# Group coefficients of the next channels between the halves of a product, and GpSimd's circuit work behind them

## The chip, the cores and the metric

The kernel runs on one core of a Trainium2 chip. The metric is the device time of one execution in microseconds (us); lower is better. Engines are named as in the profile: PE is TensorE (matmuls; PEld its weight loads), DVE is VectorE, ACT is ScalarE, POOL is GpSimd, and SP is the engine that issues most of the loads. L299 is line 299 of the kernel.

## The reference

Four residual layers are applied to x of shape (4, 512, 32, 32), each on a group-normalized input: attention with mixed heads, a gate per channel from a small simulated circuit of rotations, a second attention, and a look-up in a memory of 2048 rows. The change concerns the first normalization and the first product of layer 0, for image 0, and constants of the circuit of layer 1.

```python
def _gn(v, G=32, eps=1e-5):
    g = v.reshape(B_, G, C_ // G, H_, W_)            # 32 groups of 16 channels
    m = jnp.mean(g, axis=(2, 3, 4), keepdims=True)
    s = jnp.var(g, axis=(2, 3, 4), keepdims=True)
    return ((g - m) / jnp.sqrt(s + eps)).reshape(v.shape)

# layer 0
x = x + _L0_conv_ref(_gn(x), ...)
#   in it: q = einsum('oc,bct->bot', w_q, xf), likewise k and v, then attention
# layer 1: y = mean of _gn(x) over the positions of each channel; 2 layers of
#   9 rotations on the 512 amplitudes of y; gate = sigmoid(q_out @ fc_w.T + fc_b)
```

Image 0 is 512 channels by 1024 positions. In the kernel the channels lie in four chunks (KC = 4) of 128 partitions. A group is 16 channels, so the coefficients of a chunk depend on that chunk alone: its products can start when its own coefficients are known.

## The kernel before

The group coefficients come from a generator in four pieces. `pin` keeps an instruction in program order with the other pinned ones; what isn't pinned may be placed elsewhere in its engine's queue by the scheduler. `small_ps` is always the same PSUM bank, shown as pt.

```python
def rsqrt(dst, src):                         # GpSimd, L124
    nc.gpsimd.tensor_tensor(dst, src, mhalf[...], ALU.pow)

def group_coeffs_parts(mean, var, tag):
    ps = small_ps(f"gps_{tag}")
    pin(nc.tensor.matmul(ps[:, 0:n], gavg, mean, start=True, stop=True))    # L140
    gm = tile_("gm")
    pin(nc.vector.tensor_copy(gm, ps[:, 0:n]))                              # L142
    yield
    dm, sq = tile_("dm"), tile_("gsq")
    nc.gpsimd.tensor_sub(dm, mean, gm)                                      # L145
    nc.gpsimd.tensor_mul(sq, dm, dm)                                        # L146
    nc.gpsimd.tensor_add(sq, sq, var)                                       # L147
    yield
    ps2 = small_ps(f"gps2_{tag}")
    pin(nc.tensor.matmul(ps2[:, 0:n], gavg, sq, start=True, stop=True))     # L150
    ve = tile_("gve")
    pin(nc.vector.tensor_scalar_add(ve, ps2[:, 0:n], GN_EPS))               # L152
    yield
    rstd = tile_("grstd")
    rsqrt(rstd, ve)                                                         # L124
    yield gm, rstd, dm
```

The first image, with the chunks of x and of w_q loaded in turn:

```python
def first():
    # ... loads of xn[:, k], w_q[:, k], then w_k and w_v
    def stats(k):
        for i in range(2):
            pin(nc.vector.bn_stats(st[:, i, :], xn[:, k, i * NB:(i + 1) * NB]))   # L292
        pin(nc.vector.bn_aggr(mv, ...))                                           # L293
        parts[k] = group_coeffs_parts(mv[:, 0:1], mv[:, 1:2], f"a0_{k}")

    def normalize(k):
        next(parts[k])                       # second matmul, + eps
        gm, rstd, dm = next(parts[k])        # power
        pin(nc.vector.tensor_scalar(xn[:, k, :], xn[:, k, :], gm, rstd,
                                    ALU.subtract, ALU.mult))                      # L299
        nc.gpsimd.tensor_mul(ybar[:, k:k + 1], dm, rstd)                          # L301

    def multiply(k):
        for m in range(2):
            for n in range(T // NB):
                pin(nc.tensor.matmul(pairs[f"mx{m}"][:, n, :],                    # L306
                    w[:, k, m * P:(m + 1) * P], xn[:, k, n * NB:(n + 1) * NB],
                    start=(k == 0), stop=(k == KC - 1)))

    stats(0)
    next(parts[0])
    next(parts[0])                           # mean; deviation and its square
    for k in range(KC):
        if k + 1 < KC:
            stats(k + 1)
        normalize(k)
        if k + 1 < KC:
            next(parts[k + 1])
            next(parts[k + 1])
        multiply(k)
    for m in range(2):
        put_q(q, m)(flat2(pairs[f"mx{m}"]))  # ScalarE copies q out, L272
    for m, at in ((2, "sc"), (3, "mx0")):
        project(w, tokens(xn), m, at, put_q(q, m))       # matmuls at L183
```

The multiplication of a chunk with w_q fills two pairs of PSUM banks, mx0 and mx1, with four matmuls of 512 columns; each shows as two instructions in the profile. The rest of q follows at L183, and then k, in the banks mx1, sc, mx0, mx1 (DVE copies k out, L373), v and the attention steps.

```python
first()
circuit()
for m, at in enumerate(("mx1", "sc", "mx0", "mx1")):
    take_k(0, m, at)
```

`circuit()` makes constants for layer 1. GpSimd's part builds `turn` (L741 to L753, by copies of the identity) and signs in `par` (L767 to L775). VectorE makes masks and angles, ScalarE `sincos` (L735), and then VectorE turns `turn` by them (`rotate`, L692 to L696) and reduces `par` to `own` (L777).

```python
nc.gpsimd.tensor_copy(turn[:, 0], ident)                                  # L741
nc.gpsimd.tensor_copy(cur[:, 0], ident)                                   # L742
# ... L744, two copies
for i in range(NP - 1):                                                   # 6 rounds
    nc.gpsimd.tensor_copy(new_v[:, :, 0], old_v[:, :, 0])                 # L751
    for t in range(2):
        nc.gpsimd.tensor_copy(new_v[:, :, 1, t], old_v[:, :, 1, 1 - t])   # L753
for i in range(NP):
    for l, m in ((0, turn[:, 0:1]), (1, turn[:, 1:3])):
        rotate(...)                                                       # VectorE
nc.gpsimd.memset(par[:, 0], 1.0)                                          # L767
for i in range(NP):                                                       # 7 rounds
    nc.gpsimd.tensor_copy(new_v[:, :, 0], old_v[:, :, 0])                 # L773
    nc.gpsimd.tensor_scalar_mul(new_v[:, :, 1], old_v[:, :, 1], -1.0)     # L774
nc.gpsimd.tensor_mul(par, par, ident...)                                  # L775
```

Of the kernel before, what the change touches and what calls it, by code (L numbers as in the profile page):

```python
# [16 lines left out]
P = 128  # L17
B = 4
C = 512
T = 1024  # L20
KC = C // P
TC = T // P
NB = 512
NH = 8
HD = C // NH
# [16 lines left out]
def fast_net(ctx: ExitStack, tc: tile.TileContext, a: dict, out: bass.AP, flag: bass.AP):  # L42
    nc = tc.nc
# [8 lines left out]
    pairs = {at: ps_a.tile([P, 2, NB], F32, tag=at, name=at) for at in ("sc", "mx0", "mx1")}  # L52
# [3 lines left out]
    def pin(ins):  # L56

        return tc.keep_in_program_order(ins)

    def small_ps(name):  # L60
        return pt_bank
# [29 lines left out]
    ident = const.tile([P, P], F32, tag="ident", name="ident")  # L91
# [29 lines left out]

    def rsqrt(dst, src):

        nc.gpsimd.tensor_tensor(  # L124
            dst, src, mhalf[:dst.shape[0], :dst.shape[1]], ALU.pow
        )


    def group_coeffs_parts(mean, var, tag):

        n = mean.shape[1]

        def tile_(name):
            return small.tile(
                [P, n], F32, tag=f"{name}{n}{tag[0]}", bufs=2, name=f"{name}_{tag}")
# [4 lines that stand above are left out]
        pin(nc.vector.tensor_copy(gm, ps[:, 0:n]))  # L142
        yield
        dm, sq = tile_("dm"), tile_("gsq")
        nc.gpsimd.tensor_sub(dm, mean, gm)  # L145
        nc.gpsimd.tensor_mul(sq, dm, dm)  # L146
        nc.gpsimd.tensor_add(sq, sq, var)  # L147
        yield
        ps2 = small_ps(f"gps2_{tag}")
        pin(nc.tensor.matmul(ps2[:, 0:n], gavg, sq, start=True, stop=True))  # L150
        ve = tile_("gve")
        pin(nc.vector.tensor_scalar_add(ve, ps2[:, 0:n], GN_EPS))  # L152
        yield
        rstd = tile_("grstd")
        rsqrt(rstd, ve)
        yield gm, rstd, dm

    def coeffs(mean, var, tag):

        found = None  # L160
        for found in group_coeffs_parts(mean, var, tag):
            if found is None:
                yield
        return found
# [6 lines left out]
    def flat2(ps):  # L171
        return ps.rearrange("p n q -> p (n q)")

    def tokens(src):
        return lambda k, n: src[:, k, n * NB:(n + 1) * NB]

    def project(w, rhs, m, at, evacuate, name="proj"):


        ps = place(at, f"{name}_{m}")  # L180
        for n in range(T // NB):
            for k in range(KC):
                pin(nc.tensor.matmul(  # L183
                    ps[:, n, :], w[:, k, m * P:(m + 1) * P], rhs(k, n),
                    start=(k == 0), stop=(k == KC - 1),
                ))
        evacuate(flat2(ps))
# [40 lines left out]
    def big(tag, name):  # L228

        return apool.tile([P, KC, T], F32, tag=tag, name=name)  # L230
# [3 lines left out]
    def eight_k(shape, name, at=None):  # L234

        if at is None:
            at = turns8[0] % 3
            turns8[0] += 1
        return apool.tile(shape, F32, tag=f"w{at}", name=name)

    def load_w(key, name, at=None):
        w = eight_k([P, KC, C], name, at)
        nc.sync.dma_start(out=w, in_=a[key])
        return w
# [26 lines left out]
    def put_q(q, m):  # L271
        return lambda ps: pin(nc.scalar.copy(q[:, m, :], ps))  # L272

    def first():

        I = img[0]
        xn = I["xn"] = big("xn", "xn_0")
        w = I["w_q"] = eight_k([P, KC, C], "w_q0_0", 0)
        for k in range(KC):
            nc.sync.dma_start(out=xn[:, k, :], in_=x_v[0, :, k, :])  # L280
            nc.sync.dma_start(out=w[:, k, :], in_=a["w_q"][:, k, :])
        I["w_k"] = load_w("w_k", "w_k0_0", 1)
        I["w_v"] = load_w("w_v", "w_v0_0", 2)
        q = I["q"] = big("q", "q0_0")
        ybar = I["ybar"] = small.tile([P, KC], F32, tag="ybar", name="ybar0")
        parts = {}

        def stats(k):
            mv = small.tile([P, 2], F32, tag="mv0", name=f"mv0_{k}")
            st = small.tile([P, 2, 6], F32, tag="bnst", name=f"st_a0_{k}")  # L290
            for i in range(2):
                pin(nc.vector.bn_stats(st[:, i, :], xn[:, k, i * NB:(i + 1) * NB]))  # L292
            pin(nc.vector.bn_aggr(mv, st.rearrange("p i s -> p (i s)")))  # L293
            parts[k] = group_coeffs_parts(mv[:, 0:1], mv[:, 1:2], f"a0_{k}")

        def normalize(k):
            next(parts[k])
            gm, rstd, dm = next(parts[k])
            pin(nc.vector.tensor_scalar(  # L299
                xn[:, k, :], xn[:, k, :], gm, rstd, ALU.subtract, ALU.mult))  # L300
            nc.gpsimd.tensor_mul(ybar[:, k:k + 1], dm, rstd)  # L301

        def multiply(k):
            for m in range(2):
                for n in range(T // NB):
                    pin(nc.tensor.matmul(  # L306
                        pairs[f"mx{m}"][:, n, :],
                        w[:, k, m * P:(m + 1) * P], xn[:, k, n * NB:(n + 1) * NB],
                        start=(k == 0), stop=(k == KC - 1),
                    ))  # L310

        stats(0)
        next(parts[0])
        next(parts[0])
        for k in range(KC):
            if k + 1 < KC:
                stats(k + 1)
            normalize(k)
            if k + 1 < KC:
                next(parts[k + 1])  # L320
                next(parts[k + 1])
            multiply(k)
        for m in range(2):
            put_q(q, m)(flat2(pairs[f"mx{m}"]))
        for m, at in ((2, "sc"), (3, "mx0")):
            project(w, tokens(xn), m, at, put_q(q, m))
# [357 lines left out]
    turn = const.tile([P, 3, P], F32, tag="turn", name="turn")  # L684
# [15 lines left out]
    def circuit():  # L700

        def from_ident(view, dims):
            m = small.tile([P, view.shape[1]], F32, tag=f"mask{view.shape[1]}", name="mask")
            pin(nc.vector.tensor_reduce(m, view, dims, ALU.add))
            return m

        m = from_ident(ident.rearrange("p (r q h) -> p q r h", r=4, q=4), AX.XY)
# [7 lines left out]
        m = from_ident(ident.rearrange("p (t x) -> p x t", t=4), AX.X)  # L715
# [22 lines left out]
        tmp = e[:, 0].rearrange("p r qq k -> p (r qq k)").rearrange(  # L738
            "p (a m q) -> p a m q", a=2, q=P)
        cur, new = turn[:, 1:3], tmp[:, 0, 0:2]  # L740
        nc.gpsimd.tensor_copy(turn[:, 0], ident)  # L741
        nc.gpsimd.tensor_copy(cur[:, 0], ident)  # L742
        for t in range(2):
            nc.gpsimd.tensor_copy(  # L744
                cur[:, 1, t * HD:(t + 1) * HD], ident[:, (1 - t) * HD:(2 - t) * HD])
        for i in range(NP - 1):
            old_v, new_v = (
                t.rearrange("p m (hi c t lo) -> p (m hi) c t lo", c=2, t=2, lo=HD >> (i + 1))
                for t in (cur, new)
            )  # L750
            nc.gpsimd.tensor_copy(new_v[:, :, 0], old_v[:, :, 0])  # L751
            for t in range(2):
                nc.gpsimd.tensor_copy(new_v[:, :, 1, t], old_v[:, :, 1, 1 - t])  # L753
            cur, new = new, cur
        assert NP - 1 == 6
        for i in range(NP):
# [7 lines left out]


        par = e[:, 1].rearrange("p r qq k -> p (r qq k)").rearrange("p (i q) -> p i q", q=P)
        nc.gpsimd.memset(par[:, 0], 1.0)  # L767
        for i in range(NP):
            old_v, new_v = (
                par[:, j].rearrange("p (hi t lo) -> p hi t lo", t=2, lo=HD >> i)  # L770
                for j in (i, i + 1)
            )
            nc.gpsimd.tensor_copy(new_v[:, :, 0], old_v[:, :, 0])  # L773
            nc.gpsimd.tensor_scalar_mul(new_v[:, :, 1], old_v[:, :, 1], -1.0)  # L774
        nc.gpsimd.tensor_mul(par, par, ident.rearrange("p f -> p () f").to_broadcast([P, NH, P]))  # L775
        own = const.tile([P, NH], F32, tag="own", name="own")
        pin(nc.vector.tensor_reduce(own, par, AX.X, ALU.add))  # L777
        for k in range(KC):
# [349 lines left out]
    def chunks(take, b):  # L1128
        return [lambda at, m=m: take(b, m, at) for m in range(KC)]
# [5 lines that stand above are left out]
# [919 lines left out]
```

## Time and profile before

| | before |
|---|---|
| time, median of 3 runs | 2778.64 us (2772.06 to 2782.84) |
| span of the profiled execution | 2776.2 us |
| busy share of the span: PE, DVE, POOL, ACT | 94%, 54%, 45%, 36% |
| mean granted TensorE clock | 0.982 |
| PE busy, 0 to 15.18 us | 1.72 us |
| PE busy, 15.18 to 36.86 us | 17.23 us |
| PE busy, 36.86 to 78.22 us | 41.36 us |
| POOL busy, 0 to 15.18 us and 15.18 to 36.86 us | 10.12 us and 8.03 us |
| DMA share, 36.86 to 78.22 us | 0.00 |

The page gives totals for the whole span; the change concerns the first 37 us, so the stretches in the table and the timeline of that part say more than the totals. In the chain that ended last, each piece is either work that the end was waiting for or a wait. A piece of an engine that doesn't use the result of the piece before it stands there because it was next in its engine's queue.

### The profile page before, as it was taken

What the parts mean: (1) busy time and instruction counts of PE and PEld (TensorE: products, weight loads), DVE (VectorE), ACT (ScalarE), POOL (GpSimd) and SP (SyncE); (2) the same over time, 40 slices, a digit from 0 to 9 for tenths busy, and PEclk for the clock granted to TensorE, in tenths of its full rate; (3) what the DMA queues carried; (4) which work ended last, traced back from release to release, by engine and by line L of the source; (5) the groups of instructions that cost most, each with busy time, mean ns of one, the idle gap of its engine ahead of it and who ended that gap; (6) DMA issues with size and microseconds to landing.
All of it is one profiled execution on the core that took longest, in us unless ns stands there. A gap on an engine that the chain in (4) does not pass through costs nothing.

```text
span 2776.2 us, 46960 instructions
## 1 busy us (share of the span) xinstructions
PE 2597.5 (94%) x18286; PEld 1178.0 (42%) x18286; DVE 1502.6 (54%) x2407; ACT 1005.8 (36%) x1128; POOL 1243.1 (45%) x1947
## 2 busy tenths in 40 slices
PE   7988998989989898989989999999999999999995
PEld 3443444545445444545433433343344334444442
DVE  4488347871578426872234224413523446888886
ACT  0466336551565426551144024214512532221210
POOL 2266415552456515553066026304601635666664
PEclk9999999999999999999999999999999999999997
DMA  2488537880687527784400030021002016766665
GB/s 77 107 209 203 139 87 212 219 216 30 165 217 207 157 80 196 194 216 175 142 3 1 31 121 1 16 73 64 1 31 91 1 35 189 217 185 215 184 185 149
DMA packets 159321, 349.82 MB, mean 126 GB/s; under 512 B 32361, under 2 KB 65129, under 8 KB 155378
## 3 DMA queue, kind: packets, MB, share of 16 engines
q1 hardware_dynamic: 86304, 167.04, 20.9%
q0 software_dynamic: 51200, 142.93, 19.1%
q10 hardware_dynamic: 21586, 36.76, 4.5%
q8 instruction: 147, 2.41, 0.4%
q14 instruction: 84, 0.69, 0.1%
HBM read 178.57 MB, written 33.69 MB: 76 GB/s over the span
## 4 chain that ended last, share of the span: by engine, by line
PE 75%; DMA 7%; ACT 6%; POOL 4%; DVE 4%; issue 2%; SPq 1%; ACTq 0%; POOLq 0%; DVEq 0%
PE at L1068 16%; PE sc L425 7%; PE mx L183 7%; PE sc_c L947 6%; PE pv L485 6%; PE pv_c L980 6%; DMA s<-ss 5%; PE pt L384 4%; ACT ss L431 4%; PE sc L183 4%; PE p L183 3%; PE v L195 3%; PE k L183 3%; PE q L183 3%; PE pt L658 3%
## 5 line engine op out<-in xcount | busy, mean ns | idle before, releaser
L458 DVE STREAM_TRANSPOSE eT<-e 128x1024 f32<-128x1024 f32 x256 | 317.4, 1242 | 275.5 <-ACT e L452 273.8
L438 POOL DMA_DIRECT2D s<-ss x512 | 259.7, 515 | 399.2 <-ACT ss L431 327.4
L1085 POOL DMA_INDIRECT got<-in_mem,ix x256 | 277.8, 1085 | 210.1 <-DVE tmx L1091 94.9
L941 ACT ACTIVATE eT<-sc_c 128x1024 f32<-128x1024 f32 x256 | 248.1, 1021 | 316.2 <-PE sc_c L947 232.8
L431 ACT COPY ss<-sc 128x1024 f32<-128x1024 f32 x256 | 258.9, 1011 | 260.3 <-PE sc L425 203.2
L474 DVE BATCH_NORM_STATS2 st<-e 128x6 f32<-128x256 f32 x1024 | 341.6, 405 | 0.0
L965 POOL TENSOR_TENSOR e<-eT 128x1024 f32<-128x1024 f32 x96 | 227.8, 2374 | 208.1 <-ACT eT L941 177.7
L425 PE MATMUL sc<-k,q 64*32 64x512 f32 x4096 | 287.6, 617 | 24.6 <-ACT ss L431 19.5
L452 ACT ACTIVATE e<-mx 128x1024 f32<-128x1024 f32 x256 | 262.5, 1028 | 69.9 <-PE mx L445 29.4
L966 DVE TENSOR_TENSOR eT<-eT,e 128x1024 f32<-128x1024 f32 x96 | 122.5, 1277 | 303.4 <-POOL e L965 303.4
L947 PE MATMUL sc_c<-q,k 64*128 64x512 f32 x1024 | 248.4, 618 | 37.7 <-ACT eT L941 9.8
L485 PE MATMUL pv<-eT,v 128*64 128x128 f32 x4096 | 256.9, 280 | 0.0
L485 PEld LDWEIGHTS pv<-eT,v 128*64 128x64 f32 x4096 | 226.7, 139 | 64.1 <-issue 62.5
L980 PE MATMUL pv_c<-eT,v 128*64 128x512 f32 x1024 | 234.5, 600 | 0.0
L445 PE MATMUL mx<-s,wmix 32*32 32x512 f32 x4096 | 159.4, 618 | 42.4 <-DMA s<-ss 40.6
L1109 DVE SCALAR_TENSOR_TENSOR acc<-got,et,acc 128x512 f32<-128x512 f32 x224 | 168.5, 752 | 8.0
L947 PEld LDWEIGHTS sc_c<-q,k 64*128 64x128 f32 x1024 | 93.2, 189 | 176.5 <-issue 74.6
L1007 DVE RECIPROCAL ri_c<-ri_c 128x512 f32<-128x512 f32 x32 | 107.0, 3345 | 96.1 <-ACT ri_c L1006 96.1
L1073 ACT COPY att<-at 128x1024 f32<-128x1024 f32 x64 | 64.8, 1012 | 217.1 <-PE at L1068 217.0
L961 POOL TENSOR_TENSOR eT<-eT 128x1024 f32<-128x1024 f32 x32 | 75.6, 2361 | 145.1 <-ACT eT L941 144.9
L561 POOL TENSOR_TENSOR o<-pv,rb 64x256 f32<-64x256 f32 x128 | 111.2, 868 | 64.6 <-ACT pv L548 57.6
L980 PEld LDWEIGHTS pv_c<-eT,v 128*64 128x64 f32 x1024 | 70.9, 138 | 156.1 <-issue 155.8
(314 smaller groups left out, 3293.2 us busy)
## 6 DMA issues: line engine op xcount, KB each, us to landing
s<-ss SPq DMA_DIRECT2D x512, 128.0 KB
s<-ss POOLq DMA_DIRECT2D x512, 128.0 KB, 4.5
rb<-r POOLq DMA_DIRECT2D x64, 128.0 KB, 5.8
o<-o SPq DMA_DIRECT2D x32, 256.0 KB
xr<-in_x ACTq DMA_DIRECT2D x32, 256.0 KB
x<-xr SPq DMA_DIRECT2D x32, 256.0 KB
xr_c<-x SPq DMA_DIRECT2D x32, 256.0 KB
x<-xr_c SPq DMA_DIRECT2D x32, 256.0 KB
```

Source lines behind the costliest of these rows:

```text
L183: pin(nc.tensor.matmul(ps[:, n, :], w[:, k, m * P:(m + 1) * P], rhs(k, n), start=(k == 0), stop=(k == KC - 1),))
L425: pin(nc.tensor.matmul(sc[m * NS:(m + 1) * NS, r, :], q[r * HD:(r + 1) * HD, m, s * NS:(s + 1) * NS], k_[r * HD:(r + 1) * HD, m, n * NB:(n ...
L431: pin(nc.scalar.copy(ss[:, :, n * NB:(n + 1) * NB], sc))
L438: pin(relays[r].dma_start(out=s2[r * KC + m::NH], in_=ss[m * NS:(m + 1) * NS, r, :]))
L452: pin(nc.scalar.activation(e[:, half].rearrange("p r qq k -> p (r qq k)"), flat2(pairs[f"mx{half}"]), AF.Exp))
L458: pin(nc.vector.transpose(eT[:, j % 2].rearrange("p b (qq i r) x -> p i r qq b x", qq=2, i=4)[:, i, 2 * half:2 * half + 2], e[:, half].rea ...
L474: pin(nc.vector.bn_stats(st[:, i, 2 * half + r, qq, :], e[:, half, r, qq, :]))
L485: pin(nc.tensor.matmul(pv[r * HD:(r + 1) * HD, gp, :], I["v"][:, t, g * HD:(g + 1) * HD], eT[:, j % 2, t, :, 4 * g:4 * g + 4], start=(t == ...
L947: pin(nc.tensor.matmul(sc[:, r, :], I["k"][r * HD:(r + 1) * HD, m, t * P:(t + 1) * P], I["q"][r * HD:(r + 1) * HD, m, n * NB:(n + 1) * NB] ...
L980: pin(nc.tensor.matmul(pv[r * HD:(r + 1) * HD, :], I["v"][:, t, h * HD:(h + 1) * HD], e[:, r, :], start=(t == 0), stop=(t == TC - 1),))
L1068: pin(nc.tensor.matmul(sc[:, n * NB:(n + 1) * NB], xn3[b][:, k, tt * P:(tt + 1) * P], memT[k][:, i0:i0 + NB], start=(k == 0), stop=(k == K ...
L1085: pin(nc.gpsimd.indirect_dma_start(out=got[:, i, :], out_offset=None, in_=a["mem"], in_offset=bass.IndirectOffsetOnAxis(ap=ix[:, i:i + 1], ...
```

## The change

The change has two parts. First, the steps of the coefficients are set in another order. Statistics run up to two chunks ahead, the mean and the deviations of a chunk one product ahead, and the second matmul, the epsilon and the power of chunk k+1 stand between the two halves (m = 0 and m = 1) of chunk k's product. The scaling of chunk k+1 can then run beside the second half. Second, all GpSimd operations of these coefficients, and all of the circuit, are pinned, so that the circuit's work comes behind the first image's on GpSimd. No operation is added or left out.

```diff
     def rsqrt(dst, src):
-        nc.gpsimd.tensor_tensor(
+        return nc.gpsimd.tensor_tensor(
 ...
         n = mean.shape[1]
+        hold = pin if n == 1 else lambda ins: ins
 ...
-        nc.gpsimd.tensor_sub(dm, mean, gm)
-        nc.gpsimd.tensor_mul(sq, dm, dm)
-        nc.gpsimd.tensor_add(sq, sq, var)
+        hold(nc.gpsimd.tensor_sub(dm, mean, gm))
+        hold(nc.gpsimd.tensor_mul(sq, dm, dm))
+        hold(nc.gpsimd.tensor_add(sq, sq, var))
 ...
-        rsqrt(rstd, ve)
+        hold(rsqrt(rstd, ve))
 ...
+        def means(k):
+            next(parts[k])
+            next(parts[k])
+
+        def deviations(k):
+            next(parts[k])
+            found[k] = next(parts[k])
+
         def normalize(k):
-            next(parts[k])
-            gm, rstd, dm = next(parts[k])
+            gm, rstd, dm = found[k]
             pin(nc.vector.tensor_scalar(
                 xn[:, k, :], xn[:, k, :], gm, rstd, ALU.subtract, ALU.mult))
-            nc.gpsimd.tensor_mul(ybar[:, k:k + 1], dm, rstd)
+            pin(nc.gpsimd.tensor_mul(ybar[:, k:k + 1], dm, rstd))
 ...
-        def multiply(k):
-            for m in range(2):
-                for n in range(T // NB):
+        def multiply(k, m):
+            for n in range(T // NB):
 ...
         stats(0)
-        next(parts[0])
-        next(parts[0])
+        means(0)
+        stats(1)
+        deviations(0)
+        means(1)
+        normalize(0)
         for k in range(KC):
+            if k + 2 < KC:
+                stats(k + 2)
+            multiply(k, 0)
             if k + 1 < KC:
-                stats(k + 1)
-            normalize(k)
+                deviations(k + 1)
+            multiply(k, 1)
             if k + 1 < KC:
-                next(parts[k + 1])
-                next(parts[k + 1])
-            multiply(k)
+                normalize(k + 1)
+            if k + 2 < KC:
+                means(k + 2)
 ...
     # circuit(): the same for L741 to L753, L767, L773 to L775
-        nc.gpsimd.tensor_copy(turn[:, 0], ident)
-        nc.gpsimd.tensor_copy(cur[:, 0], ident)
+        pin(nc.gpsimd.tensor_copy(turn[:, 0], ident))
+        pin(nc.gpsimd.tensor_copy(cur[:, 0], ident))
 ...
```

More of the change, by code (lines that the diff above doesn't have):

```diff
@@ L285, in first @@
         ybar = I["ybar"] = small.tile([P, KC], F32, tag="ybar", name="ybar0")
-        parts = {}
+        parts, found = {}, {}
         def stats(k):
@@ L294, in stats @@
             parts[k] = group_coeffs_parts(mv[:, 0:1], mv[:, 1:2], f"a0_{k}")
+        def means(k):
[4 more added lines that the diff above has]
+            found[k] = next(parts[k])
         def normalize(k):
-            next(parts[k])
-            gm, rstd, dm = next(parts[k])
+            gm, rstd, dm = found[k]
             pin(nc.vector.tensor_scalar(
                 xn[:, k, :], xn[:, k, :], gm, rstd, ALU.subtract, ALU.mult))
-            nc.gpsimd.tensor_mul(ybar[:, k:k + 1], dm, rstd)
-        def multiply(k):
-            for m in range(2):
-                for n in range(T // NB):
[L306 to L310, printed above, removed]
-        stats(0)
-        next(parts[0])
-        next(parts[0])
+            pin(nc.gpsimd.tensor_mul(ybar[:, k:k + 1], dm, rstd))
+        def multiply(k, m):
+            for n in range(T // NB):
+                pin(nc.tensor.matmul(
+                    pairs[f"mx{m}"][:, n, :],
+                    w[:, k, m * P:(m + 1) * P], xn[:, k, n * NB:(n + 1) * NB],
+                    start=(k == 0), stop=(k == KC - 1),
+                ))
+        stats(0)
+        means(0)
[3 more added lines that the diff above has]
+        normalize(0)
         for k in range(KC):
+            if k + 2 < KC:
+                stats(k + 2)
+            multiply(k, 0)
             if k + 1 < KC:
-                stats(k + 1)
-            normalize(k)
+                deviations(k + 1)
+            multiply(k, 1)
             if k + 1 < KC:
-                next(parts[k + 1])
-                next(parts[k + 1])
-            multiply(k)
+                normalize(k + 1)
+            if k + 2 < KC:
+                means(k + 2)
         for m in range(2):
@@ L740, in circuit @@
         cur, new = turn[:, 1:3], tmp[:, 0, 0:2]
-        nc.gpsimd.tensor_copy(turn[:, 0], ident)
-        nc.gpsimd.tensor_copy(cur[:, 0], ident)
+        pin(nc.gpsimd.tensor_copy(turn[:, 0], ident))
+        pin(nc.gpsimd.tensor_copy(cur[:, 0], ident))
         for t in range(2):
-            nc.gpsimd.tensor_copy(
-                cur[:, 1, t * HD:(t + 1) * HD], ident[:, (1 - t) * HD:(2 - t) * HD])
+            pin(nc.gpsimd.tensor_copy(
+                cur[:, 1, t * HD:(t + 1) * HD], ident[:, (1 - t) * HD:(2 - t) * HD]))
         for i in range(NP - 1):
@@ L750, in circuit @@
             )
-            nc.gpsimd.tensor_copy(new_v[:, :, 0], old_v[:, :, 0])
+            pin(nc.gpsimd.tensor_copy(new_v[:, :, 0], old_v[:, :, 0]))
             for t in range(2):
-                nc.gpsimd.tensor_copy(new_v[:, :, 1, t], old_v[:, :, 1, 1 - t])
+                pin(nc.gpsimd.tensor_copy(new_v[:, :, 1, t], old_v[:, :, 1, 1 - t]))
             cur, new = new, cur
@@ L766, in circuit @@
         par = e[:, 1].rearrange("p r qq k -> p (r qq k)").rearrange("p (i q) -> p i q", q=P)
-        nc.gpsimd.memset(par[:, 0], 1.0)
+        pin(nc.gpsimd.memset(par[:, 0], 1.0))
         for i in range(NP):
@@ L772, in circuit @@
             )
-            nc.gpsimd.tensor_copy(new_v[:, :, 0], old_v[:, :, 0])
-            nc.gpsimd.tensor_scalar_mul(new_v[:, :, 1], old_v[:, :, 1], -1.0)
-        nc.gpsimd.tensor_mul(par, par, ident.rearrange("p f -> p () f").to_broadcast([P, NH, P]))
+            pin(nc.gpsimd.tensor_copy(new_v[:, :, 0], old_v[:, :, 0]))
+            pin(nc.gpsimd.tensor_scalar_mul(new_v[:, :, 1], old_v[:, :, 1], -1.0))
+        pin(nc.gpsimd.tensor_mul(par, par, ident.rearrange("p f -> p () f").to_broadcast([P, NH, P])))
         own = const.tile([P, NH], F32, tag="own", name="own")
```

## The prediction, written before the result was known

> **What bounds the kernel now.** I read the slices of the page first (TensorE busy 94% of the span, its worst stretches at the start and between images), then the chain that ended last, in order of time, for the first 40 us, because the diff touches only that stretch and the circuit behind it. The columns are start (us), length (us), what.
>
> ```profile
> 0.81 4.97 DMA xn<-in_x
> 5.79 1.30 DVE st_a L292 x2
> ...
> 8.30 0.19 POOL dm_a L145
> 8.50 0.17 POOL e L773
> 8.67 0.36 POOL e L774
> 9.03 0.17 POOL gsq_a L146
> 9.20 0.23 POOL turn L751
> 9.42 0.15 POOL gsq_a L147
> ...
> 13.41 0.33 POOL e L774
> 13.74 0.55 POOL grstd_a L124
> ...
> 14.32 0.82 DVE xn L299
> ...
> 15.18 5.17 PE mx L306 x8
> 20.35 0.14 PE pt L150 x2
> 20.52 0.17 DVE gve_a L152
> ...
> 20.75 0.59 POOL grstd_a L124
> 21.37 0.82 DVE xn L299
> ...
> 22.24 3.70 PE mx L306 x8
> ```
>
> Two things are to be seen. First, between the mean of chunk 0 and its power the chain runs through the circuit's copies (L751, L753, L773, L774), which chunk 0 does not need: they merely stand in front of L146, L147 and L124 in GpSimd's queue. The power starts at 13.74, though its input, gve of chunk 0 (L152), was written at 10.41 by the timeline. Second, after each chunk's products TensorE stops, and one after the other come the second group matmul, the epsilon add, the power and the scaling of 1024 columns, before the next chunk's products can start. The timeline has the products of the four chunks at 15.18, 22.24, 27.78 and 33.32, and the stream behind them (q, third part) at 36.86.
>
> What follows is a solid block of matmuls. In the chain from there:
>
> ```profile
> 33.32 3.70 PE mx L306 x8
> 37.02 6.87 PE sc L183 x16
> 43.89 13.73 PE mx L183 x32
> 57.62 6.87 PE sc L183 x16
> 64.49 13.73 PE mx L183 x32
> 78.22 3.43 PE pt L384 x8
> ```
>
> From 37.02 to 81.65 nothing but TensorE is on the chain: an earlier start there is an earlier arrival in the attention of image 0.
>
> **What the Trainium skill says.** "PSUM — Partial Sum Buffer", Engine vs sequencer instructions: the queues of ScalarE, VectorE and GpSimd are strict first-in first-out. The lines above agree: L146 waits about 0.5 us behind two circuit operations although dm was there at 8.49. "TensorE: Matmul & The Clock Gate", What's actually happening: the array starts at half clock and comes to full clock after about 3.4 us of sustained work, in a free-running window. The trace agrees roughly: the eight matmul instructions of chunk 0 take 5.17 us, those of chunk 1 take 3.70, and the weight loads go from 0.34 to 0.19 us at about 18.5, 3.3 us after 15.18. "SBUF — State Buffer", Who interferes with whom: VectorE in a two-port mode and GpSimd lock each other out of a shared port. One line fits: ybar of chunk 0 took 0.68 us beside the 0.81 us scaling, against 0.19 in the three other chunks. It is off the chain both before and after.
>
> **The change, part 1: chunk 0.** Pinning puts all GpSimd work of the first image ahead of the circuit. Nothing changes up to dm (8.30). With nothing between, the three small operations start 0.27 us apart, as those of chunk 2 do (22.33, 22.60, 22.87), so the square is complete at 8.30 + 0.27 + 0.27 + 0.19 = 9.03 instead of 9.57. The second group matmul then runs 9.08 to 9.66 (0.58 in the timeline). VectorE still does chunk 1's statistics here and its aggregate ends at 9.76; then the epsilon add (0.16) ends at about 9.95, and the power (0.58) runs from 10.0 to 10.6. Meanwhile the mean matmul of chunk 1, now ahead of chunk 0's products, takes 10.0 to 10.6 and its copy to 10.8. This copy stands before the scaling in VectorE's queue and costs about 0.15. Scaling 10.8 to 11.6, products at about **11.65 instead of 15.18: 3.5 us earlier**. The data are there: x chunk 1 was already waiting at 8.23, and by the DMA view everything of the first three chunks had landed by about 12.2, the fourth chunk's issue coming at 12.39.
>
> **Part 2: the three gaps.** Start to start, the products now cost 7.06, 5.54, 5.54 and 3.54 us, together 21.68. The last, 3.54, has no gap behind it; so the bare products are 3.54 for a warm chunk and about 5.01 for the cold one (15.18 to the small matmul's start at 20.19): 5.01 + 3 x 3.54 = 15.63. The gaps are the other 6.05 us. In the changed order the circle for chunk k+1 starts between the two halves of chunk k. From the end of the small matmul it needs: epsilon add 0.04 + 0.16, power 0.07 + 0.56, scaling 0.04 + 0.81, hand-over 0.05, together 1.73 us. Beside it run the second half of the products (half of 3.54, 1.77) and the mean matmul of chunk k+2. So it is **just hidden**, with nothing to spare but that matmul. The statistics are spread one chunk further ahead: 1.27 + 0.21 us on VectorE start after the mean copy and are done some 1.6 us later, before the epsilon add of that round comes due, so VectorE doesn't hold up the circle.
>
> What stays on TensorE: five pairs of group matmuls stand in the stream (second matmul of chunks 1 to 3, mean of chunks 2 and 3). One pair shows 0.28 us, and the weight loads around so short a matmul (0.19 each) can't hide; I estimate 0.4 us each, 2.0 us in all. New length 15.63 + 2.0 = 17.63 instead of 21.68: **4.0 us saved**. The stream behind starts at 11.65 + 17.63 = 29.3 instead of 36.86: **7.5 us earlier in all**.
>
> **Part 3: the circuit, later.** GpSimd's part (L741 to L775) is about 12 us of busy time by its groups. It now begins after ybar of chunk 3, about 26. The part making turn, 1.0 us of first copies and six rounds of 0.6 to 0.8, is done at about 31.5. VectorE's rotations wait for sincos as well, now from 39.38 behind the two q copies and a table load of 1.28; with the copies 7.5 earlier that is about 32. So turn is there in time, if narrowly, and the rest (about 7.5 us: seven pairs at 0.7, then 2.34 for L775) ends near 39, before own asks for it (13 us after the rotations begin). VectorE's circuit work, 39.65 to about 54.3 now, would end near 47, still before the copy of k's first part at 29.3 + 3 x 6.87 = 49.9. Even a delay of 5 us would only hold up that copy; its PSUM bank is wanted again two products later, 13.7 us on. **Cost: none.**
>
> **The sum.** 7.5 us off the start, all else shifted. The three runs have the median 2778.6; 2778.6 - 7.5 = **2771 us**, 0.27%.
>
> **The rivals.** *Only the first part comes.* If a half of the products is too short to cover the circle, or the mean copies and statistics get in front of it on VectorE, each round keeps a gap of 0.5 to 1 us, and the gain is 3.5 plus 1 to 2.5: 2773 to 2774. For it: cover of 1.77 against a circle of 1.73. Against it: the mean matmul adds cover. *GpSimd's late circuit becomes a wait.* It would have to arrive over 15 us late to reach TensorE; the 12 us of work speaks against it. Time then 2771 to 2775. *The clock takes part back.* The half-clock phase is a length of time; if its window falls worse after the earlier small matmuls, chunk 0 costs up to 1 us more, if better, 1 us less. Later, where TensorE pauses between images (granted clock 0.93 at 200 to 300 us, 0.97 around 1300 us), a shift can move such phases either way; that's in the 10.8 us between the fastest and slowest of the three runs. *The gain is absorbed later*, by a transfer that starts at a fixed time: speaking against it, the queues are idle from 36.86 to 78.22 (DMA share 0.00) and all later loads are issued relative to the steps. *Another order elsewhere*: the unpinned instructions of layer 2 could be placed differently by the scheduler. I see no reason in the diff, but can't exclude a few us.
>
> **Range and chances.** The mechanism gives 5 to 8.5 us; a median of few runs adds about 4 on each side. So 2764 to 2778. 2% is 56 us, more than all of the first 37 us: within 2% has 0.98.
>
> **What would show it.** Right: in the chain, products of chunk 0 near 11.65 with no L751 or L774 ahead of L124; the products of the four chunks with gaps under 0.5 us; q's third part near 29.3; DVE's rotations near 32; the steps of image 0 all about 7.5 us earlier. Part 1 is wrong if products start after 12.5, part 2 if the rows of L306 still show idle time until the scaling of more than 1 us in sum over chunks 1 to 3, part 3 if L692 waits for GpSimd's turn or a matmul for the copy of k. The whole is wrong if the start comes 7 us earlier, but the steps from 100 us on do not, or if the time rises beyond 2780.

## The result and the profile after

| | before | after |
|---|---|---|
| time, median of 6 runs each | 2780.18 us | 2766.85 us |
| lowest to highest | 2772.06 to 2782.9 | 2763.75 to 2773.07 |
| span of the profiled execution | 2776.2 us | 2766.7 us |
| products of chunk 0 start | 15.18 us | 11.73 us |
| third part of q on the chain | 37.02 us | 28.73 us |

The ratio is 0.9959, 95% interval 0.994 to 0.9978: faster by 6 to 17 us, 0.41%, where 0.27% had been predicted. The chain of the changed kernel in order of time (start, length in us, what; L313 is the old L306, L307 the old L299, L184 the old L183):

```profile
8.48 1.30 DVE st_a L293 x2
...
10.17 0.60 PE pt L141 x2
...
10.95 0.73 DVE xn L307
...
11.73 3.70 PE mx L313 x4
15.43 0.12 PE pt L151 x2
15.54 1.82 PE mx L313 x4
...
17.48 1.82 PE mx L313 x4
...
23.30 5.43 PE mx L313 x12
28.73 6.87 PE sc L184 x16
```

GpSimd is gone from this part of the chain, and from 11.73 to 79.24 us it is TensorE alone. The table by stretches says the same: the first column after the stretch is its length, the next PE's busy time.

```profile
11.73:28.57 16.84, 16.84 (x43) 7.87 (x44) 8.87 (x28) 2.29 (x2) 7.85 (x31) 1.00 0.52 179
28.57:69.93 41.36, 41.36 (x98) 18.52 (x97) 21.64 (x54) 4.55 (x5) 8.41 (x22) 1.00 0.00 1
```

Before, the products took 21.68 us, with PE busy for 17.23 of them; now they take 16.84, and PE is busy for all of it. The solid block behind them is 41.36 us in both. The circuit, now late on GpSimd, holds nobody up (timeline of GpSimd and VectorE):

```profile
31.43 0.29 DVE L705 TENSOR_SCALAR e<-turn,sincos 128x128 f32<-128x128 f32 x1 [3.21 <-ACT sincos L748]
35.20 2.40 POOL L788 TENSOR_TENSOR e<-e,ident 128x1024 f32<-128x1024 f32 x1
49.37 1.93 DVE L386 COPY k<-mx 128x1024 f32<-128x1024 f32 x1 [1.04 <-PE mx L184]
```

VectorE's rotations wait for sincos, not for turn; the last GpSimd operation ends at 37.6, and own asks for it at 46.66; the copy of k waits for its matmuls and not for the circuit.

I matched the two traces matmul by matmul. The same matmul comes 8.29 us earlier from 40 us to 150 us; from 150 to 1700 us the median of this shift over 50 us walks between 5.7 and 10.5, and from 1750 to 2700 us it stays at 9.4. In the built programs no engine's order differs behind the first stage, and the two traces show the same: behind the first image's coefficients and the circuit every engine runs the same instructions in the same order. So nothing was placed elsewhere by the scheduler.

### The profile page after: what moved, and what is told of

Read it like the earlier page. It is cut to its first block, busy times and chain, and to the rows that moved or that the text cites. A ratio compares the mean times of both kernels' runs of the same rounds, so it can differ in the third digit from the quotient of the medians.

```text
span 2766.7 us, 46961 instructions
## 1 busy us (share of the span) xinstructions
PE 2599.8 (94%) x18286; PEld 1180.6 (43%) x18286; DVE 1508.2 (55%) x2407; ACT 1005.4 (36%) x1128; POOL 1247.4 (45%) x1947
## 4 chain that ended last, share of the span: by engine, by line
PE 76%; DMA 7%; ACT 6%; POOL 4%; DVE 3%; issue 3%; SPq 1%; ACTq 1%; POOLq 0%; DVEq 0%
PE at L1081 16%; PE sc L438 7%; PE mx L184 7%; PE pv L498 6%; PE sc_c L960 6%; PE pv_c L993 6%; PE pt L397 4%; DMA s<-ss 4%; PE sc L184 4%; ACT ss L444 4%; PE p L184 3%; PE v L196 3%; PE q L184 3%; PE k L184 3%; PE pt L671 3%
```

## Experiments

In the list below, "start" is the third part of q on the chain against 37.02, the one profile of before; the time is the mean of a kernel's runs less the mean of the runs of before on the same chip, with its 95% interval. Single runs of one kernel scatter with a standard deviation of 4 to 5.5 us in most groups.

| kernel | start | time, us | runs, of before |
|---|---|---|---|
| changed kernel, first time | -8.29 | -11.5 +- 4.7 | 6, 6 |
| changed kernel, again | -7.54 | -12.0 +- 2.5 | 6, 59 |
| changed kernel, third time | -8.06 | -11.0 +- 3.3 | 9, 34 |
| changed kernel, fourth time | -6.85 | -9.9 +- 3.0 | 11, 16 |
| order alone | -3.74 | -4.8 +- 2.8 | 20, 59 |
| pins alone | -3.08 | -2.5 +- 2.7 | 20, 59 |
| third part of q twice | -1.20, by the fourth part | -1.9 +- 2.4 | 22, 59 |
| nine small matmuls ahead | -7.78 | -8.2 +- 2.7 | 16, 36 |
| the same, x in halves | -8.20 | -8.8 +- 2.3 | 22, 36 |
| chunk 0 first | -7.48 | -8.4 +- 2.8 | 21, 34 |
| chunk 0 first, pauses filled | -10.02 | -8.8 +- 2.9 | 11, 34 |

### The order alone, the pins alone

Order alone takes back all the pins:

```diff
-        hold = pin if n == 1 else lambda ins: ins
+        hold = lambda ins: ins
-            pin(nc.gpsimd.tensor_mul(ybar[:, k:k + 1], dm, rstd))
+            nc.gpsimd.tensor_mul(ybar[:, k:k + 1], dm, rstd)
     # and circuit() as before
```

> The new order of the steps alone; none of GpSimd's work on the coefficients or the circuit is pinned, so the circuit's copies stand among the coefficients again. Theory (two separate gains that add up: 3.5 us from the queue in chunk 0, the rest from the gaps): the power of chunk 0 waits for the copies as before, its products start near 15.3 us instead of 11.7, the halves then follow each other without gaps, and the third part of q starts near 32.2 us (36.86 before, 28.57 with the whole change); time about 4.6 us under before. Rival (the order is worth nothing while GpSimd's queue is in the way): the circuit's multiplication of 2.34 us stands ahead of the power of chunk 1, gaps of some 2 us remain, and the third part of q starts at 34 us or later.

Pins alone has `normalize`, `multiply` and the loop as before, with all pins.

> The pinning alone, in the old order of steps. Theory: the products of chunk 0 start near 11.6 us, the three gaps of about 2 us each stay, and the third part of q starts near 33.3 us; time about 3.6 us under before. Rival (the gaps come from GpSimd's queue too): gaps shrink below 1.5 us and the third part of q starts before 32 us.

Chain of the order alone, then of the pins alone:

```profile
13.31 0.33 POOL e L787
13.64 0.55 POOL grstd_a L124
...
15.08 3.78 PE mx L313 x4
...
19.07 2.84 PE mx L313 x4
...
33.28 6.87 PE sc L184 x16
```

```profile
11.72 5.58 PE mx L307 x8
...
17.69 0.57 POOL grstd_a L124
...
18.29 0.82 DVE xn L300
...
19.16 3.70 PE mx L307 x8
...
33.94 6.87 PE sc L184 x16
```

With the order alone, the power of chunk 0 stands behind L787 as before, but no pause is left between the halves, though the circuit's copies still lie in GpSimd's queue. With the pins alone the products start at 11.72 and the pauses stay, 1.84 to 1.86 us each. So there are two gains, one from each part: 3.7 and 3.1 us in the start, 6.8 together, against 6.9 to 8.3 in the four profiles of the whole. Both rivals are out by what they forecast. Of the first one, the premise came true: the circuit's multiplication (2.35 us from 17.23) did stand ahead of the power of chunk 1, which started at 19.53, 0.26 us after its epsilon and not the usual 0.07. It cost nothing, since the second half beside it took 2.84 us instead of 1.82, still in part at half clock. For the same reason the order alone came 0.9 us later than expected: 33.12 by the timeline, in which the expected 32.2 was reckoned too.

### What a small matmul costs in the stream

```diff
-        pin(nc.tensor.matmul(ps2[:, 0:n], gavg, sq, start=True, stop=True))
+        for _ in range(2 if tag in ("a0_1", "a0_2", "a0_3") else 1):
+            pin(nc.tensor.matmul(ps2[:, 0:n], gavg, sq, start=True, stop=True))
     # likewise the mean matmul of a0_2 and a0_3
```

> The changed kernel with the five small matmuls inside the stream of products each issued twice (second matmul of chunks 1 to 3, mean of chunks 2 and 3), which measures what one of them costs there. Theory (a pair and the loads around it cost 0.22 us: the changed kernel's warm halves start 1.94 us apart, where four instructions of 0.43 are 1.72): the halves start 2.16 us apart, 1.1 us more over all five. Rival (0.4 us each, as the prediction had it): the halves start 2.3 to 2.4 us apart, 2 us more over all five.

The chain of this kernel, which ran once:

```profile
18.12 1.82 PE mx L315 x4
...
20.29 1.82 PE mx L315 x4
```

The halves start 2.16 to 2.17 us apart, against 1.94 in the changed kernel: **a pair costs 0.22 us**, not 0.4.

### How closely the circle is covered

```diff
-        hold(rsqrt(rstd, ve))
+        for _ in range(2 if tag in ("a0_1", "a0_2", "a0_3") else 1):
+            hold(rsqrt(rstd, ve))
```

> The changed kernel with the power of chunks 1 to 3 computed twice on GpSimd, which lengthens the circle of epsilon, power and scaling by about 0.57 us. Theory (the circle of 1.73 us is just covered by half a product and a mean matmul, 1.94, and by 1.72 for the last chunk): waits for the scaling appear ahead of the products of chunks 1 to 3, 0.3 to 0.4 us for chunks 1 and 2 and 0.5 to 0.6 for chunk 3, 1.2 us in sum. Rival (there is more room than it seems, because scaling and products overlap): no wait, third part of q at the same distance from the first product.

TensorE's timeline, with the idle time and its releaser in brackets:

```profile
18.16 1.98 PE L314 MATMUL mx<-xn,w_q 128*128 128x512 f32 x4 [0.33 <-DVE xn L308]
22.62 1.99 PE L314 MATMUL mx<-xn,w_q 128*128 128x512 f32 x4 [0.41 <-DVE xn L308]
27.07 3.70 PE L314 MATMUL mx<-xn,w_q 128*128 128x512 f32 x8 [0.53 <-DVE xn L308]
```

This kernel too ran once. The waits are there, 1.27 us in sum, in the sizes expected. In the changed kernel the scaling of chunk 1 ends at 17.22 and its products start at 17.34: the cover holds with about 0.1 us to spare. For chunk 3, with no mean matmul beside its circle, it is already too short: its first matmul instruction starts 0.49 us after the one before, where the stream has 0.43. Little of a further operation is hidden, then. The three added powers are 1.9 us (0.63 each, start to start). By the timeline it takes 18.81 us from the first product to the third part of q, against 17.12 in the third profile of the changed kernel, whose chunk 0 ran alike: 1.7 of the 1.9 us reach the stream. The brackets sum to less because a matmul's modelled end lies 0.14 to 0.16 us behind the point at which the next could start.

### Does a later start move the end?

```diff
+        project(w, tokens(xn), 2, "sc", lambda ps: None)
         for m, at in ((2, "sc"), (3, "mx0")):
             project(w, tokens(xn), m, at, put_q(q, m))
```

> The changed kernel, with the third part of q computed twice over (16 matmul instructions, 6.87 us by the chain), so that all behind it starts later by a known amount; the first copy of it is thrown away. Theory (a start moved by x moves the end by x, and what goes beyond that comes from the clock's half-speed windows): the first product of k starts 6.87 us later than in the changed kernel, and the end lies 6.9 us later, give or take 3; time about 1.4 us under before. Rival (the end gains more than the start did because a later wait got shorter, or a later wait takes up changes of the start): the time stays within 2 us of the changed kernel.

The fourth part of q came at 42.69 on the chain, 43.89 before: 1.2 us ahead. The time lies 1.9 (+- 2.4) under before; of the gain of the changed kernel nearly all is lost with the 6.9 us put in. Against the changed kernel's six runs on the same chip the loss is 10.1 us (+- 2.8), at the edge of the 6.9, give or take 3; against all its 32 runs it is 8.1 (+- 2.3). The rival, by which the time wouldn't follow the start, is out.

### The changed kernel again

> The changed kernel once more, on the same chip as the three others. Theory (8.3 us from the start, the rest of the first difference from the half-speed windows of TensorE's clock, which fall differently in every run): third part of q near 28.6 us again; time 8 us under before, give or take 4, and the shift between the two traces moves up and down by 1 to 3 us in the stretch from 150 to 1300 us where such windows lie. Rival (some 3 to 5 us more are gained regularly behind the start): time 11 to 13 us under before, with a shift that settles at the same place along the trace as it did the first time.

> The changed kernel a third time, for the size of the whole difference. Theory (the end moves with the start, as the runs with one part alone and with the doubled third part of q showed): 7.5 to 8.5 us under before in the mean of many runs. Rival (3 us more are gained regularly behind the start): 10.5 us under before or more.

> The changed kernel a fourth time. So far its time lies 10.6 us (give or take 1.8) under before in the mean, though its third part of q starts only 7.5 to 8.3 us earlier; in seven other kernels with the same changes in parts, or with more of them, the end moved as the start did, within 1.2 us each. Theory (the extra 2.6 us are chance, from half-speed windows that fall differently in every run): about 8 us under before, and the mean of all its runs comes closer to 8. Rival (the changed kernel gains something of its own behind the start): again 10.5 us or more under before.

All 32 runs together lie 10.2 us (+- 1.5) under the 151 runs of before (11.2 +- 1.6 with each group set against its own runs of before, weighted), while the start is 7.7 us earlier in the mean of four profiles. By the time, the second and third run came out on the rival's side and the fourth between the two (its medians are 7.3 apart). By the traces they didn't: the shift against before ends at 9.4, 9.1, 13.0 and 14.5 us in the four, and it grows at other places in each. Neither theory nor rival is settled by this.

### Towards a better start

First, nine matmuls of 128 columns ahead of the products, to bring up TensorE's clock, and then x of chunk 0 in two loads besides:

```diff
         stats(0)
+        warm(8)      # matmuls of gavg with gavg into a bank not yet in use
         means(0)
+        warm(1)
```

> The changed kernel with nine matmuls of 128 columns added on TensorE ahead of its first products (eight before the mean of chunk 0, one after; their result is not used). Theory (the first half of chunk 0's products takes 3.5 us instead of 1.72 only because TensorE had been idle, and is at half clock): that half takes 1.8 to 2 us, nothing else becomes a limit before 15.5 us, and the third part of q starts near 26.7 us instead of 28.6; time about 2 us below the changed kernel, 10 us under before. Rival (the small matmuls with pauses between don't bring the clock up, or the statistics of chunk 2, whose data land at about 12.2 us, hold up the next chunk instead): third part of q at 28 us or later.

> The same with x of chunk 0 loaded in two halves, so that its statistics can begin before all of it is there. Theory (until the first product the chain is the load of chunk 0, its statistics and the circle): the first statistics start about 0.7 us earlier, the second follow the landing, and the products start 0.4 to 0.7 us earlier than with the nine matmuls alone; third part of q near 26.2 us. Rival (the load is bound by what the queue moves in all, and the extra issue delays the later chunks): no gain, or a wait for x of chunk 2 or w_q takes it.

```profile
8.53 0.38 PE L151 MATMUL pt<-gsq_a,gavg 128*128 128x1 f32 x2 [0.73 <-POOL gsq_a L148]
10.25 0.59 PE L141 MATMUL pt<-mv,gavg 128*128 128x1 f32 x2 [1.34 <-DVE gve_a L153]
11.81 3.78 PE L313 MATMUL mx<-xn,w_q 128*128 128x512 f32 x4 [0.97 <-DVE xn L307]
```

That is TensorE's timeline with nine matmuls: at 8.53 a pair takes 0.38 us, at 10.25 again 0.59, and the first half its 3.78. The clock had come up and fell back, so the first theory fails. The rival's start came (29.24), though not for its reason: the small matmuls did bring the clock up, but it didn't last until the products. With x in halves, the statistics of chunk 0 start at 4.29 instead of 5.49, yet the products only at 11.27 instead of 11.81, since chunk 1's x lands at 8.08 and VectorE has chunk 1's statistics ahead of chunk 0's epsilon. This wait was in all but the first profile of the changed order; here from the second profile of the changed kernel:

```profile
8.65 1.29 DVE L293 BATCH_NORM_STATS2 st_a<-xn 128x6 f32<-128x512 f32 x2 [0.66 <-DMA xn<-in_x]
```

So chunk 0 went first, with x in halves, and then with TensorE's pauses filled as well:

```diff
         stats(0)
+        warm(8)                      # pauses filled only
         means(0)
-        stats(1)
+        warm(2)                      # pauses filled only
         deviations(0)
-        means(1)
+        warm(4)                      # pauses filled only
         normalize(0)
+        stats(1)
+        multiply(0, 0)
+        means(1)
+        multiply(0, 1, (0,))         # first quarter
+        deviations(1)
+        multiply(0, 1, (1,))
+        stats(2)
+        normalize(1)
+        means(2)
-        for k in range(KC):
+        for k in range(1, KC):       # as in the changed kernel
```

> The changed kernel with three more moves: x of chunk 0 is loaded in two halves; chunk 0's epsilon, power and scaling come ahead of chunk 1's statistics on VectorE, so that they no longer wait for x of chunk 1, which lands at 8.1 to 9.1 us; chunk 1's mean stands behind the first half of chunk 0's products. Theory (what sets the first product after the change is x of chunk 1, through VectorE's queue): first product near 9.6 us instead of 11.8, third part of q near 26.5 us instead of 28.6 to 29.5; time 2 to 3 us below the changed kernel. Rival (x of chunk 1 and 2 then set the second and third chunk's products just as late): first product near 9.6 us, third part of q still at 28 us or later.

> The same, with small matmuls of 128 columns (8, 2 and 4 of them) in TensorE's pauses until the first product. Theory (in the run with nine of them the clock had come up by 7 us and fell back in the pauses from 8.9 to 11.8 us; with the pauses filled it stays up): first half of chunk 0's products in 1.8 us instead of 3.4 to 3.8, third part of q 0.5 to 1.5 us earlier than without them, limited by the landing of x of chunks 1 and 2. Rival (small matmuls don't keep the clock up): that half again 3.4 us or more and no gain.

Without the filling the products start at 9.88 but the third part of q only at 29.54. I had set the statistics of chunk 2 ahead of chunk 1's scaling on VectorE; the chain shows them (15.96, 1.20 us) between epsilon and scaling, and TensorE was at half clock besides. The rival was right about the third part of q, but not for its reason: x of chunk 2 was there. With the pauses filled, TensorE's timeline has

```profile
9.69 1.98 PE L322 MATMUL mx<-xn,w_q 128*128 128x512 f32 x4 [0.76 <-DVE xn L312]
```

1.98 us instead of 3.78, and the third part of q comes at 27.00, 1.7 us ahead of the earliest of the changed kernel's four. The statistics of chunk 2 stand ahead of chunk 1's scaling here too (13.43, 1.20 us), and TensorE is idle for 0.72 and 0.29 us just before chunk 1's products, so this isn't yet the earliest start. The time, 8.8 us (+- 2.9) under before, can't be told from the changed kernel's 10.2 (+- 1.5). It starts earlier; that it is faster isn't shown.

## Why the prediction was right, step by step

The time of 2766.85 us lies in the range of 2764 to 2778, below the 2771 named.

**GpSimd's queue in chunk 0: right.** Products at 11.73 instead of 15.18, 11.65 named; the pins alone brought it about. What the prediction missed is the next limit. It took x of chunk 1 as present at 8.23, as the trace of before had it. In ten later profiles of kernels with that order of VectorE's queue it landed between 8.08 and 9.06 us, and VectorE waited for it, with chunk 0's epsilon behind. In the first profile of the changed kernel there was no such wait. In the second, chunk 0's second matmul was done at 9.44 and its epsilon came only at 10.09: what was gained by an earlier landing of chunk 0 (statistics at 5.55 instead of 6.04) went into this wait of 0.66 us. That the products start at 11.68 to 11.86 in all four profiles, so close to the 11.65, is in part luck.

**The three gaps: right.** They closed with the new order alone, and the cover is as close as the 1.73 against 1.77 us said: about 0.1 us in the trace, a little less than nothing for chunk 3, and one more power shows nearly in full. In the first profile this part is worth 4.84 us (21.68 less 16.84), 4.0 named; in the other three 3.54 to 4.56.

**What stays on TensorE: mis-sized terms, in opposite directions.** The five pairs cost 0.22 us each, not 0.4, 0.9 us less in all. The chunk at half clock took 5.17 us on the chain before; after, its two halves took 3.70 + 1.82 = 5.52 in the first profile, and 5.69 to 6.73 in the other three of the same kernel. By the timeline, which the prediction used, the third part of q starts at 28.57, 29.32, 28.80 and 30.00 in the four, 29.2 in the mean, with 29.3 predicted. That the two errors nearly cancel is luck.

**The circuit costs nothing: right.** Rotations at 31.43 (32 named), no wait for GpSimd.

**The whole sum: the start is shown, the rest isn't.** Eight kernels in the table (the doubled pairs and powers ran once each) set the end against the start; in seven of them, all but the changed kernel itself, the time moved within 1.3 us of the start, on either side. The changed kernel gained 2.5 us (+- 1.5) more than its start, an interval that leaves out the scatter of the four starts. All starts are set against the one profile of before. If another profile of it had its chunk 0 longer than 5.17 us, as the four of the changed kernel differ among themselves, all eight kernels would shift alike, so that doesn't single out this one. Of the rivals, another order elsewhere is excluded by the order of the built programs. The clock was named as the one that can move phases either way, and the traces show that it does: all but 0.6 us of the shift's changes come between 150 and 1750 us, where TensorE's clock is at half speed for 71.7 us in all in the profile of before (up to 2700 us) and for 81.9, 75.1, 78.5 and 64.9 us in the four of the changed kernel. But the difference in these sums doesn't explain a gain of 2.5 us: the first profile ended 9.4 us ahead with more half-speed time than before. Whether this rest is chance, or something of the changed kernel that its close relatives don't have, stays open.

## What to carry to other kernels

Ahead of a long block that is bound by one engine, look at what stands in front of the first needed result in each engine's queue, and at where each small circle through other engines could run beside a half of the work. Both gains were there and added up. When such a wait is taken away, look in several profiles for the next one in the same queue (here a load behind VectorE's statistics), since one trace shows only how it fell that time. Below half a per cent, read gains from the trace, where the start scattered by 1.4 us over four profiles, and take tens of runs for the time.

## What the runs showed of the hardware that was not expected

- TensorE's clock came up under small matmuls and went back within a few microseconds of sparse work. With nine of them (first two lines) TensorE was busy for 1.42 of 3.41 us, with no pause over 0.81 us, and then at half clock; with the pauses filled (last line) it was busy for 2.28 of 3.41 us and stayed up. The second figure after the stretch is PE's busy time, the third from the end the granted clock:

```profile
5.94:9.35 3.41, 1.42 (x9) 0.95 (x8) 1.92 (x6) 0.00 (x0) 0.57 (x3) 1.00 0.83 235
9.35:12.76 3.41, 1.54 (x3) 1.00 (x4) 2.05 (x6) 0.00 (x0) 1.79 (x5) 0.50 0.73 239
6.14:9.55 3.41, 2.28 (x18) 1.90 (x17) 1.04 (x3) 0.00 (x0) 1.35 (x5) 1.00 0.70 219
```

- The Trainium skill, "TensorE: Matmul & The Clock Gate", What's actually happening, has free-running windows of about 3.4 us, and a fall to half clock after an idle one. The half-speed stretches of all profiles, but for the one at the end, are whole numbers of 3.41 us, on a raster whose place differed from run to run. The window ahead of the fall was not idle here, though: 1.42 us of work in it didn't hold the clock.
- The same raster makes the first products uneven: chunk 0's two halves took 5.52, 6.08, 5.69 and 6.73 us in four profiles of one kernel, and in the same order the trace has the clock's rise to full speed 3.5, 4.8, 4.0 and 6.1 us after the first product. The 3.3 us that the prediction read in the trace of before is one such case.
- A GpSimd operation of 128x1 that takes 0.19 us alone took 0.69 when it started 0.16 us after VectorE's scaling (dm of chunk 1, at 11.03), as ybar did before, 0.18 us after it. Both ended about 0.05 us after the scaling. Being beside the scaling is not enough: ybar of chunks 1 to 3, before and after, starts 0.04 us after it and takes 0.19, so the prediction's comparison with these three was not one of alone against beside. The square behind dm was ready at 12.26, and wanted only at 15.26.
